# Attention in steps of two: maxima subtracted by four 32-row matmuls, and score banks shared in turn

## The chip, the cores and the metric

The kernel runs on one core of a Trainium2 chip. A core has five engines that run side by side, each with its own queue executed in program order: TensorE (PE) multiplies matrices, VectorE (DVE) and ScalarE (ACT) do arithmetic and read TensorE's results, GpSimd (POOL) does arithmetic on SBUF, SyncE (SP) starts DMAs. Results of TensorE land in PSUM, which has eight banks of 128 partitions x 512 float32 numbers. The metric is the device time of one launch in microseconds (us), median of several runs.

## The reference

The reference has two layers on an input of shape (4, 128, 64, 64), float32. Layer 0 is attention over the 4096 positions of each image, with 4 heads of width 32, followed by a residual and a layer norm over the channels. Layer 1 sums a 3x3 convolution, a spectral 1x1 convolution (through a 2-D Fourier transform) and a selective scan ("Mamba": 256 inner channels, 16 states).

```
Q, K, V = split_heads(x_flat @ W + b)
attn = softmax(einsum("bhnd,bhmd->bhnm", Q, K) * head_dim ** -0.5)
y = layernorm((attn @ V merged) @ Wo + bo + x_flat)
out = conv3x3(y) + spectral(y) + mamba(y)
```

The change is in how the softmax's scores are formed: the row maximum has to be known before the exponential is taken, so the kernel forms all scores twice, once to find the maxima and once, with the maximum subtracted, for the exponential.

## The kernel before

**Tiles.** The positions of an image are cut into 8 chunks of 512 queries. A "half" H is one chunk of queries with one pair of heads, so there are 64 halves. Within a half there are 32 steps, one for each block of 128 keys. That makes 2048 steps in all, and time in the kernel's program is counted in these steps (`t`).

**One step** issues, in this order:

- `scores_for_exp`(H, m), line 486: scores of 128 keys x 512 queries for both heads of the pair, into a tile of two PSUM banks (tag `s2`, one buffer). Each head has its own bank and its own 64 rows of TensorE's array, so the two heads' matmuls stand side by side. Three such pairs of matmuls are summed: queries in a low and a high part (K times Q), then the negated maximum, added by a matmul of `sel` (ones in two rows of each head's 64) with `MX`, which holds the negated maxima in a high and a low part in those two rows. ScalarE takes the exponential of the two banks at once (line 502).
- `scores_for_max`(H + 1, s), line 442: scores of 128 queries x 512 keys for the next half, two pairs of matmuls into two banks (tag `s1`, one buffer), reduced to a maximum per query by VectorE (line 461). It runs `LEAD` = 7 steps ahead of the next half's first exponential.
- `times_values`(H, m - 1), line 505: the exponentials of the step before times V, for the two heads in two column halves of the array, summed in one bank (tag `o`). These are plain float32 and each takes two instructions.

After the last step of a half, ScalarE and VectorE each copy one head's sums out of the bank (`oz`, lines 524 and 525). `maxima` (line 463) takes the last maximum over the parts, splits it, writes it to `wide` and has TensorE transpose it into `MX`.

**Side work.** Projections, the layer norm, the convolution, the spectral part and the scan of earlier chunks run in the gaps. `Plan` (line 102) holds them as jobs that give way at each need: P for a place on TensorE, D on VectorE, A on ScalarE, B for one of two shared PSUM banks (`m0`, `m1`). `plan.step` is called once per step with the number of places; before the change a step with an odd number gives two places of each kind and an even one gives one to ScalarE only. The scan is issued outside the planner: in every second step one state is scanned by VectorE (`scan_state`, line 834), with its decay from ScalarE (`scan_decay`, line 821, into a bank of its own) and its products on GpSimd (lines 832, 854, 873). When the attention is over, a remainder of the scan runs alone.

PSUM is full: two banks for `s1`, two for `s2`, and one each for `o`, `dA`, `m0`, `m1`. A tile with one buffer can be written again only when its reader is done.

The loop that sets the order is the last of the function, from line 1062:

```
if 0 <= H < HALVES:
    scores_for_exp(H, m)
h1, s1 = divmod(t + LEAD, NT)
if 0 <= h1 + 1 < HALVES:
    scores_for_max(h1 + 1, s1)
...
plan.step(t, {"D": 2, "P": 2, "A": 2})
...
if not last and 0 <= H < HALVES:
    times_values(H, m)
```

Of the kernel before, what the change touches and what calls it, by code (L numbers as in the profile page):

```python
# [9 lines left out]
F32 = mybir.dt.float32  # L10
F32R = mybir.dt.float32r
AF = mybir.ActivationFunctionType
ALU = mybir.AluOpType
# [4 lines left out]
P = 128  # L18
W = 64
HEADS = 4  # L20
HD = P // HEADS
PAIRS = HEADS // 2
HS = P // 2
L = 512
RPC = L // W
TPC = L // P
# [25 lines left out]
def _constants():  # L52

    w = np.arange(W)
    k = np.arange(1, W // 2)
    sin = np.sin(2 * np.pi * np.outer(w, k) / W).sum(1) * 2 / W
    hil = sin[(w[:, None] - w[None, :]) % W]
    c = np.zeros((P, NCONST), np.float64)
    c[:, K_ID : K_ID + P] = np.eye(P)  # L70
    for r in range(2):
        s = slice(r * W, (r + 1) * W)
        c[s, K_HIL + r * W : K_HIL + (r + 1) * W] = hil.T
    c[:, K_G : K_G + W] = -sin
    for j in range(2):
        c[j * HS, K_SEL : K_SEL + P] = 1.0
        c[j * HS + HD, K_SEL : K_SEL + P] = 1.0
    c[2 * DTR : 4 * DTR, K_LO] = -1.0
    for j in range(2):
        c[(2 * j + 1) * DTR : (2 * j + 2) * DTR, K_LO + 1] = -1.0  # L80
    return c.astype(np.float32)
# [80 lines left out]
def attention_then_conv_mamba(  # L162
# [153 lines left out]
    ]  # L316
    VA = [const.tile([P, TPC, HEADS, HD + 1], F32, name=f"V_{i}") for i in range(NCH)]

    wide = const.tile([P, TPC, 2, HS], F32, name="wide")
    nc.gpsimd.memset(wide, 0.0)  # L320
    state = const.tile([P, NH * NS], F32, name="state")
    carry = const.tile([P, NH, TAPS - 1], F32, name="carry")
# [119 lines left out]
    def scores_for_max(H, s):  # L442

        k = H % PAIRS
        m, t = divmod(s, TPC)
        assert have["K", k, m] == H // PAIRS // NCH
        if s == 0:
            part[H] = att.tile([P, TPC, 2, NCH], F32, tag="part", name=f"part_{H}")

        tag = "s2" if H == 0 and s % 2 else "s1"  # L450
        sc = psum.tile([P, 2, L], F32, tag=tag, name=f"s1_{H}_{s}")
        for n in range(2):
            for j in range(2):
                nc.tensor.matmul(  # L454
                    sc[:, j, :],
                    QT[H][rows[j], n, t * P : (t + 1) * P],
                    KK[k][m][rows[j], :],
                    start=n == 0,
                    stop=n == 1,
                )  # L460
        nc.vector.tensor_reduce(part[H][:, t, :, m], sc, AX.X, ALU.max)  # L461

    def maxima(H):

        yield "D"
        mx = att.tile([P, TPC, 2], F32, tag="mx", name=f"mx_{H}")
        nc.vector.tensor_reduce(mx, part.pop(H), AX.X, ALU.max)
        hi = att.tile([P, TPC, 2], F32R, tag="mhi", name=f"mhi_{H}")
        nc.vector.tensor_scalar(hi, mx, -1.0, None, ALU.mult)
        nc.vector.tensor_copy(wide[:, :, :, 0], hi)  # L470
        nc.vector.scalar_tensor_tensor(wide[:, :, :, HD], mx, -1.0, hi, ALU.mult, ALU.subtract)
        yield ""
        bank = yield "PB"
        pm = bank_tile(bank, [P, L], f"pm_{H}")
        for t in range(TPC):
            nc.tensor.transpose(
                pm[:, t * P : (t + 1) * P], wide[:, t].rearrange("p j d -> p (j d)"), ident
            )
        yield "A"
        plan.release(bank)  # L480
        MX[H] = att.tile([P, L], F32R, tag="MX", name=f"MX_{H}")
        nc.scalar.activation(MX[H], pm, AF.Copy)
# [2 lines left out]

    def scores_for_exp(H, m):

        k = H % PAIRS
        i, t = divmod(m, TPC)
        assert have["K", k, i] == H // PAIRS // NCH  # L490
        s = psum.tile([P, 2, L], F32, tag="s2", name=f"s2_{H}_{m}")
        for n, mov in enumerate((QT[H][:, 0, :], QT[H][:, 1, :], MX[H])):
            for j in range(2):
                nc.tensor.matmul(  # L494
                    s[:, j, :],
                    sel[rows[j], :] if n == 2 else KK[k][i][rows[j], t * P : (t + 1) * P],
                    mov[rows[j], :],
                    start=n == 0,
                    stop=n == 2,
                )  # L500
        e = att.tile([P, 2, L], F32, tag="e", name=f"e_{H}_{m}", bufs=3)
        nc.scalar.activation(e, s, AF.Exp)  # L502
        es[H, m] = e

    def times_values(H, m):

# [314 lines left out]
    def scan_decay(c, v):  # L821
        n, hf = divmod(v, NH)
        k = hf * NS + n

        tag = "o" if plan.t >= HALVES * NT + 2 and v % 2 else "dA"
        dA[c, v] = psum.tile([P, L], F32, tag=tag, name=f"dA_{c}_{k}")
        nc.scalar.activation(dA[c, v], dts[c][hf], AF.Exp, scale=negA[:, k : k + 1])  # L827

    def scan_input_term(c, v, engine):
        n, hf = divmod(v, NH)  # L830
        db[c, v] = loc.tile([P, L], F32, tag="db", name=f"db_{c}_{hf * NS + n}")
        engine.tensor_tensor(db[c, v], us[c][hf], bcs[c, n][0], ALU.mult)  # L832

    def scan_state(c, v):

        n, hf = divmod(v, NH)
        k = hf * NS + n
        assert (c, hf) in scaled
        late = plan.t > HALVES * NT + 1
        if late:  # L840
            hs = flat(VA[v % 4])
        else:
            hs = loc.tile([P, L], F32, tag="hs", name=f"hs_{c}_{k}")
        nc.vector.tensor_tensor_scan(  # L844
            hs,
            dA.pop((c, v)),
            db.pop((c, v)),
            state[:, k : k + 1] if c % NCH else zero,
            ALU.mult,
            ALU.add,  # L850
        )
        if c % NCH < NCH - 1:
            nc.gpsimd.tensor_copy(state[:, k : k + 1], hs[:, L - 1 :])  # L853
        nc.gpsimd.tensor_tensor(hs, hs, bcs[c, n][1], ALU.mult)  # L854
        if hf == NH - 1 and (c, n) in taken:
            spare.append((plan.t + 6, taken.pop((c, n))))
        elif hf == NH - 1:
            ring[0] += 1
        if late:

            if c not in sums_late:
                sums_late[c] = psum.tile(
                    [P, NH, L], F32, tag=f"s{1 + c % 2}", name=f"acc_{c}"
                )
            terms = [hs] if n else [xss[c][hf], hs]
            for x in terms:
                waiting.append((plan.t + 4, c, hf, x, n == NS - 1 and x is hs))
        elif n == 0:
            acc = loc.tile([P, L], F32, tag=f"acc{hf}", name=f"acc_{c}_{hf}")
            accs[c, hf] = acc  # L870
            nc.gpsimd.tensor_tensor(acc, xss[c][hf], hs, ALU.add)
        else:
            nc.gpsimd.tensor_tensor(accs[c, hf], accs[c, hf], hs, ALU.add)  # L873
# [149 lines left out]

    LEAD = 7
    SLOT = PAIRS * NT
    LAG = 2 * SLOT + 16
    STATES = NH * NS
# [26 lines left out]
        for i in range(NCH // 2):  # L1056
            plan.at((b + 1) * NCH * SLOT + 44 + 10 * i, 4, flips(b * NCH + NCH // 2 - 1 - i))

    t = 6 - SLOT
    loaded = 0  # L1060
    end = (CHUNKS + 3) * SLOT
    while t < end or not plan.idle():
        H, m = divmod(t, NT)
        if 0 <= H < HALVES:
            scores_for_exp(H, m)
        h1, s1 = divmod(t + LEAD, NT)
        if 0 <= h1 + 1 < HALVES:
            scores_for_max(h1 + 1, s1)
        H, m = divmod(t - 1, NT)
        last = m == NT - 1  # L1070
        if last and 0 <= H < HALVES:
            times_values(H, m)
        c, s = divmod(t - LAG, SLOT)
        odd = s % 2 == 1
        if -1 <= c < CHUNKS:
            v = c * STATES + s // 2
            if not odd:
                if v >= 0:
                    scan_state(*divmod(v, STATES))
            else:  # L1080
                if 0 <= v + 1 < CHUNKS * STATES:
                    scan_decay(*divmod(v + 1, STATES))
                if 0 <= v + 2 < CHUNKS * STATES:
                    late = t > HALVES * NT
                    scan_input_term(
                        *divmod(v + 2, STATES), nc.vector if late else nc.gpsimd
                    )

                if loaded < CHUNKS * NS and loaded // NS in bcds:
                    if ring[0] or spare and spare[0][0] <= t:  # L1090
                        scan_load(*divmod(loaded, NS))
                        loaded += 1
        plan.late = t > HALVES * NT
        if plan.late:
            add_states()
            if odd:
                plan.step(t, {"D": 4, "P": 4, "A": 6})
            plan.t = t
        elif t < -LEAD:
            plan.step(t, {"D": 4, "P": 4, "A": 4})  # L1100
        elif odd:
            plan.step(t, {"D": 2, "P": 2, "A": 2})
        else:
            plan.step(t, {"D": 0, "P": 0, "A": 1})
        if not last and 0 <= H < HALVES:
            times_values(H, m)
        t += 1


# [74 lines left out]
```

## Time and profile before

| | us |
|---|---|
| median of 3 runs | 6039.58 (6039.44 to 6041.75) |
| the profiled execution | 6038.33 |
| its span | 6036.5 |
| TensorE busy | 5847.1 (97%) |
| VectorE busy | 4360.0 (72%) |
| ScalarE busy | 3586.6 (59%) |
| GpSimd busy | 4482.6 (74%) |
| attention: first to last matmul of L494 and L514 | 128.5 to 5817 |

A group in the profile is all instructions of one line, engine and tile; "idle before" is the time the engine stood still just before them. A wait line reads "engine line <- engine line waited for: us in total, times, longest". A timeline row has start, length, engine, line, operation, out<-in and how many instructions it merges. A matmul's recorded length overlaps that of the next, so intervals between starts tell more than lengths. The granted clock of TensorE is full (1.00) from 300 to 5700 us.

### The profile page before, as it was taken

The numbers are of one execution on the slowest core, as the hardware profiler recorded it, in microseconds if no ns is written. First come the engines' busy times: TensorE is split into PE (matmuls) and PEld (weight loads), VectorE is DVE, ScalarE is ACT, GpSimd is POOL, SyncE is SP. The second block draws the span as 40 slices with busy tenths as digits, with TensorE's granted clock in tenths as the row PEclk, the third lists the DMA queues.
The fourth block names the chain that finished last, engine by engine and source line by source line (L and its number), as shares of the span: only waits on it lengthen the run. The fifth ranks groups of instructions, "written<-read, shape, count | busy, mean of one in ns | idle before, by whom it ended". The sixth has DMA issues, their size and how long they took to land. (4 is left out here: it accounts for less than half of the span.)

```text
span 6036.5 us, 82731 instructions
## 1 busy us (share of the span) xinstructions
PE 5847.1 (97%) x31382; PEld 2443.1 (40%) x31382; DVE 4360.0 (72%) x4569; ACT 3586.6 (59%) x4826; POOL 4482.6 (74%) x4522
## 2 busy tenths in 40 slices
PE   5999999999999999999999999999999999999976
PEld 2444444444444444444444444444444444444422
DVE  4557777777777777777777777777777777777657
ACT  1455666666666666666666666666666666666653
POOL 0006888778887778888788888777888887888877
PEclk7999999999999999999999999999999999999988
DMA  4012222224333223223432222322433222222233
GB/s 125 25 36 58 65 71 75 71 70 110 82 89 73 73 72 74 72 64 89 104 84 82 74 68 71 75 68 73 108 75 92 67 67 63 66 71 63 62 98 89
DMA packets 266641, 455.28 MB, mean 75 GB/s; under 512 B 46688, under 2 KB 48256, under 8 KB 266240
## 3 DMA queue, kind: packets, MB, share of 16 engines
q1 hardware_dynamic: 261584, 448.11, 28.1%
q8 instruction: 246, 4.03, 0.3%
q10 hardware_dynamic: 4656, 1.87, 0.1%
q14 instruction: 155, 1.27, 0.1%
HBM read 375.68 MB, written 65.80 MB: 73 GB/s over the span
## 5 line engine op out<-in xcount | busy, mean ns | idle before, releaser
L461 DVE TENSOR_REDUCE part<-s 128x2 f32<-128x1024 f32 x2048 | 2498.1, 1221 | 1411.4 <-PE s L454 1407.6
L502 ACT ACTIVATE e<-s 128x1024 f32<-128x1024 f32 x2048 | 2095.5, 1023 | 2121.6 <-PE s L494 2117.0
L514 PE MATMUL po<-e,V 128*33 128x512 f32 x8192 | 2180.9, 605 | 2.4 <-DVE oz L525 0.3
L494 PE MATMUL s<-Q,K 64*128 64x512 f32 x8192 | 1501.0, 444 | 13.5 <-ACT e L502 10.2
L454 PE MATMUL s<-K,Q 64*128 64x512 f32 x8192 | 1308.9, 397 | 41.4 <-DVE part L461 32.3
L854 POOL TENSOR_TENSOR hs<-hs,bc 128x512 f32<-128x512 f32 x948 | 1211.0, 1277 | 170.3 <-DVE hs L844 101.3
L494 PEld LDWEIGHTS s<-Q,K 64*128 64x128 f32 x8192 | 610.2, 185 | 1736.3 <-ACT e L502 1237.0
L832 POOL TENSOR_TENSOR db<-u,bc 128x512 f32<-128x512 f32 x948 | 1215.6, 1282 | 0.0
L873 POOL TENSOR_TENSOR acc<-acc,hs 128x512 f32<-128x512 f32 x894 | 1145.4, 1281 | 70.1
L844 DVE TENSOR_TENSOR_SCAN hs<-dA,state,db 128x512 f32<-128x512 f32 x826 | 1052.8, 1275 | 41.9 <-ACT dA L827 40.1
L454 PEld LDWEIGHTS s<-K,Q 64*128 64x128 f32 x8192 | 750.1, 185 | 294.9 <-DVE part L461 129.4
L494 PE MATMUL s<-MX,sel 64*128 64x512 f32 x4096 | 808.0, 391 | 0.0
L827 ACT ACTIVATE dA<-dt,negA 128x512 f32<-128x512 f32 x1024 | 703.2, 687 | 115.7 <-DVE V L844 69.5
L853 POOL COPY state<-hs 128x1 f32<-128x1 f32 x858 | 157.9, 184 | 789.8 <-DVE hs L844 786.0
L514 PEld LDWEIGHTS po<-e,V 128*33 128x33 f32 x8192 | 305.4, 109 | 886.5 <-issue 840.8
L494 PEld LDWEIGHTS s<-MX,sel 64*128 64x128 f32 x4096 | 383.9, 185 | 90.7
L928 PE MATMUL pf<-xp,cw 128*128 128x512 f32 x576 | 288.2, 618 | 0.0
L558 POOL TENSOR_TENSOR op<-op,rz 128x512 f32<-128x512 f32 x32 | 41.4, 1294 | 178.6 <-DMA rz<-rd 175.8
L844 DVE TENSOR_TENSOR_SCAN hs<-dA,zero,db 128x512 f32<-128x512 f32 x128 | 163.2, 1275 | 0.9 <-POOL db L832 0.7
L880 PE MATMUL acc<-V,cst 128*128 128x512 f32 x140 | 95.0, 783 | 63.6 <-POOL V L854 63.5
L928 PEld LDWEIGHTS pf<-xp,cw 128*128 128x128 f32 x576 | 96.8, 189 | 119.6 <-issue 117.9
L712 POOL TENSOR_TENSOR xs<-xs,sg_x 128x512 f32<-128x512 f32 x64 | 81.8, 1279 | 79.3 <-ACT sg_x L636 79.3
(147 smaller groups left out, 3571.2 us busy)
## 6 DMA issues: line engine op xcount, KB each, us to landing
bc<-bcd SPq DMA_DIRECT2D x487, 512.0 KB
Q<-qd SPq DMA_DIRECT2D x256, 128.0 KB
K<-kd SPq DMA_DIRECT2D x64, 256.0 KB
K<-bcd SPq DMA_DIRECT2D x42, 256.0 KB
vd<-vst SPq DMA_DIRECT2D x32, 264.0 KB
V<-vd SPq DMA_DIRECT2D x32, 264.0 KB
xq<-in_x SPq DMA_DIRECT2D x32, 256.0 KB
xk<-in_x SPq DMA_DIRECT2D x32, 256.0 KB
```

The lines of the kernel that those rows point to most:

```text
L454: nc.tensor.matmul(sc[:, j, :], QT[H][rows[j], n, t * P : (t + 1) * P], KK[k][m][rows[j], :], start=n == 0, stop=n == 1,)
L461: nc.vector.tensor_reduce(part[H][:, t, :, m], sc, AX.X, ALU.max)
L494: nc.tensor.matmul(s[:, j, :], sel[rows[j], :] if n == 2 else KK[k][i][rows[j], t * P : (t + 1) * P], mov[rows[j], :], start=n == 0, stop= ...
L502: nc.scalar.activation(e, s, AF.Exp)
L514: nc.tensor.matmul(po[H][used[j], :], VA[i][:, t, 2 * k + j, :], e[:, j, :], start=m == 0, stop=m == NT - 1,)
L827: nc.scalar.activation(dA[c, v], dts[c][hf], AF.Exp, scale=negA[:, k : k + 1])
L832: engine.tensor_tensor(db[c, v], us[c][hf], bcs[c, n][0], ALU.mult)
L844: nc.vector.tensor_tensor_scan(hs, dA.pop((c, v)), db.pop((c, v)), state[:, k : k + 1] if c % NCH else zero, ALU.mult, ALU.add,)
L853: nc.gpsimd.tensor_copy(state[:, k : k + 1], hs[:, L - 1 :])
L854: nc.gpsimd.tensor_tensor(hs, hs, bcs[c, n][1], ALU.mult)
L873: nc.gpsimd.tensor_tensor(accs[c, hf], accs[c, hf], hs, ALU.add)
L928: nc.tensor.matmul(pf, cw[:, k, :], xps[c][:, dy : dy + RPC, dx : dx + W], start=k == 0, stop=False)
```

## The change

Two steps are issued together. `scores_for_exp` fills two tiles: the scores of the first step, then four matmuls of 32 rows each that add the negated maxima (`sel` now has ones in the first two rows of each 32; `wide` and so `MX` hold the high and low part in each quarter), then the scores of the second step. Quarter q = 0 of each head goes to the first tile and closes its sum, q = 1 goes to the second tile and opens its sum. The tags `s1` and `s2` become `s0` and `s1`, and maxima scores and exponential scores of even steps share `s0`, those of odd steps `s1`. The loop is written anew for pairs of steps: both exponentials, the values of the step before, the maxima scores of the even step, side work with places for TensorE, the maxima scores of the odd step, the values, side work with places for VectorE, then the scan. `LEAD` is 8.

```diff
-    for j in range(2):
-        c[j * HS, K_SEL : K_SEL + P] = 1.0
-        c[j * HS + HD, K_SEL : K_SEL + P] = 1.0
+    for r in range(P // HD):
+        c[r * HD : r * HD + 2, K_SEL : K_SEL + P] = 1.0
...
-    wide = const.tile([P, TPC, 2, HS], F32, name="wide")
+    wide = const.tile([P, TPC, 2, 2, HD], F32, name="wide")
...
-        tag = "s2" if H == 0 and s % 2 else "s1"
-        sc = psum.tile([P, 2, L], F32, tag=tag, name=f"s1_{H}_{s}")
+        sc = psum.tile([P, 2, L], F32, tag=f"s{s % 2}", name=f"s1_{H}_{s}")
...
-        nc.vector.tensor_copy(wide[:, :, :, 0], hi)
-        nc.vector.scalar_tensor_tensor(wide[:, :, :, HD], mx, -1.0, hi, ALU.mult, ALU.subtract)
+        high, low = (wide[:, :, :, :, k] for k in range(2))
+        mx2, hi2 = (v.unsqueeze(3).to_broadcast([P, TPC, 2, 2]) for v in (mx, hi))
+        nc.vector.tensor_copy(high, hi2)
+        nc.vector.scalar_tensor_tensor(low, mx2, -1.0, hi2, ALU.mult, ALU.subtract)
...
+        both = [
+            psum.tile([P, 2, L], F32, tag=f"s{r}", name=f"s2_{H}_{m + r}") for r in range(2)
+        ]
+        for r in range(2):
+            i, t = divmod(m + r, TPC)
+            for n in range(2):
+                for j in range(2):
+                    nc.tensor.matmul(
+                        both[r][:, j, :],
+                        KK[k][i][rows[j], t * P : (t + 1) * P],
+                        QT[H][rows[j], n, :],
+                        start=n == 0 and r == 0,
+                        stop=n == 1 and r == 1,
+                    )
+            if r == 0:
+                for j in range(2):
+                    for q in range(2):
+                        quarter = slice(j * HS + q * HD, j * HS + (q + 1) * HD)
+                        nc.tensor.matmul(
+                            both[q][:, j, :],
+                            sel[quarter, :],
+                            MX[H][quarter, :],
+                            start=q == 1,
+                            stop=q == 0,
+                        )
+            e = att.tile([P, 2, L], F32, tag="e", name=f"e_{H}_{m + r}", bufs=3)
+            nc.scalar.activation(e, both[r], AF.Exp)
+            es[H, m + r] = e
...
-    LEAD = 7
+    LEAD = 8
...
+    for t in range(6 - SLOT, ATTENTION + 2, 2):
+        plan.t = t
+        if 0 <= t < ATTENTION:
+            scores_for_exp(*divmod(t, NT))
+        values(t - 1)
+        max_scores(t)
+        decay(t)
+        early = t < -LEAD
+        plan.step(t, {"D": 4, "P": 4, "A": 4} if early else {"D": 0, "P": 2, "A": 1})
+        max_scores(t + 1)
+        values(t)
+        plan.step(t + 1, {"D": 4, "P": 4, "A": 4} if early else {"D": 2, "P": 0, "A": 2})
+        scan(t)
+        prepare(t + 1, nc.gpsimd)
...
+    while not plan.idle() or t < (CHUNKS + 3) * SLOT:
+        plan.t = t
+        decay(t)
+        scan(t)
+        add_states()
+        decay(t + 2)
+        prepare(t + 1, nc.vector)
+        add_states()
+        plan.step(t + 1, {"D": 4, "P": 4, "A": 6})
+        t += 2
```

More of the change, by code (lines that the diff above doesn't have):

```diff
@@ L476, in maxima @@
             nc.tensor.transpose(
-                pm[:, t * P : (t + 1) * P], wide[:, t].rearrange("p j d -> p (j d)"), ident
+                pm[:, t * P : (t + 1) * P], wide[:, t].rearrange("p j r d -> p (j r d)"), ident
             )
@@ L488, in scores_for_exp @@
         k = H % PAIRS
[L489 to L503, printed above, removed]
+        both = [
[3 more added lines that the diff above has]
+            i, t = divmod(m + r, TPC)
+            assert have["K", k, i] == H // PAIRS // NCH
+            for n in range(2):
[21 more added lines that the diff above has]
+            es[H, m + r] = e
     def times_values(H, m):
@@ L862, in scan_state @@
                 sums_late[c] = psum.tile(
-                    [P, NH, L], F32, tag=f"s{1 + c % 2}", name=f"acc_{c}"
+                    [P, NH, L], F32, tag=f"s{c % 2}", name=f"acc_{c}"
                 )
@@ L1057, in attention_then_conv_mamba, with decay, scan, prepare @@
             plan.at((b + 1) * NCH * SLOT + 44 + 10 * i, 4, flips(b * NCH + NCH // 2 - 1 - i))
-    t = 6 - SLOT
     loaded = 0
[L1061 to L1065, printed above, removed]
+    decayed = -1
+    def decay(t):
+        nonlocal decayed
+        v = (t - LAG) // 2
+        if 0 <= v < CHUNKS * STATES and v > decayed:
+            scan_decay(*divmod(v, STATES))
+            decayed = v
+    def scan(t):
+        v = (t - LAG) // 2
+        if 0 <= v < CHUNKS * STATES:
+            scan_state(*divmod(v, STATES))
+    def prepare(t, engine):
+        nonlocal loaded
+        v = (t - LAG) // 2 + 2
+        if 0 <= v < CHUNKS * STATES:
+            scan_input_term(*divmod(v, STATES), engine)
+        if loaded < CHUNKS * NS and loaded // NS in bcds:
+            if ring[0] or spare and spare[0][0] <= t:
+                scan_load(*divmod(loaded, NS))
+                loaded += 1
+    def max_scores(t):
         h1, s1 = divmod(t + LEAD, NT)
@@ L1068, in attention_then_conv_mamba, with values @@
             scores_for_max(h1 + 1, s1)
-        H, m = divmod(t - 1, NT)
-        last = m == NT - 1
-        if last and 0 <= H < HALVES:
+    def values(t):
+        H, m = divmod(t, NT)
+        if 0 <= H < HALVES:
             times_values(H, m)
[L1073 to L1107, printed above, removed]
+    ATTENTION = HALVES * NT
@@ L1111 @@
+    plan.late = True
+    t = ATTENTION + 2
+    while not plan.idle() or t < (CHUNKS + 3) * SLOT:
[8 more added lines that the diff above has]
+        t += 2
 def kernel(**inputs):
```

## The prediction, made before the changed kernel ran

> **What bounds the kernel now.** I read the busy table first, then the groups and the waits, then the timeline of one step. TensorE is 97% busy, but a matmul's ends are modelled, so I ask who waits for whom.
>
> ```profile
> PE 5847.1 (97%) x31382; PEld 2443.1 (40%) x31382; DVE 4360.0 (72%) x4569; ACT 3586.6 (59%) x4826; POOL 4482.6 (74%) x4522
> ...
> ACT e L502 <- PE s L494: 2117.0, 1860, 9.7
> DVE part L461 <- PE s L454: 1407.6, 860, 11.3
> ...
> PE s L454 <- DVE part L461: 32.3, 62, 1.5
> ```
>
> ScalarE and VectorE wait thousands of microseconds for TensorE's scores. TensorE waits 32 us in all for VectorE. So TensorE's own queue sets the pace of the attention, and I price that queue matmul by matmul. The timeline (start, length, engine, line) shows one step without side work, then one with a matmul of 32 rows:
>
> ```profile
> 3007.25 0.73 PE L494 MATMUL s<-Q,K 64*128 64x512 f32 x4
> 3007.82 0.39 PE L494 MATMUL s<-MX,sel 64*128 64x512 f32 x2
> 3008.05 0.62 PE L454 MATMUL s<-K,Q 64*128 64x512 f32 x4
> 3008.61 1.05 PE L514 MATMUL po<-e,V 128*33 128x512 f32 x4
> 3009.59 0.50 PE L494 MATMUL s<-Q,K 64*128 64x512 f32 x2
> ...
> 3663.46 0.63 PE L454 MATMUL s<-K,Q 64*128 64x512 f32 x4
> 3664.02 0.72 PE L742 MATMUL pdt<-dtr,dtw 32*128 32x512 f32 x2
> 3664.67 1.05 PE L514 MATMUL po<-e,V 128*33 128x512 f32 x4
> ```
>
> Starts, not lengths, are what counts. A pair of 64-row matmuls side by side ("a pass") takes 0.23 (3007.82 to 3008.05). Two passes before a change of shape take 0.56 (3008.05 to 3008.61), so 0.10 is lost at the change. Two passes just after a change take 0.57: 0.11 is a weight load that could not go ahead. The values take 0.98. A clean step is 2.34. L742 is the key row: two matmuls on 32 rows, following 64-row ones. The change to it costs the usual 0.10 (3663.46 to 3664.02 is 0.56), and its own two matmuls take 0.65 = 2 x 0.23 + 0.10 for the load + 0.10 for the next change. So going from 64 to 32 rows is a full change of shape, worth about 0.20.
>
> VectorE matters too. These are its reductions at the start, where nothing but they and the maxima's matmuls run, and one clean step:
>
> ```profile
> 85.69 0.73 PE L454 MATMUL s<-K,Q 64*128 64x512 f32 x4 [0.27 <-DVE part L461]
> 86.82 0.73 PE L454 MATMUL s<-K,Q 64*128 64x512 f32 x4 [0.40 <-DVE part L461]
> ...
> 3008.32 1.02 ACT L502 ACTIVATE e<-s 128x1024 f32<-128x1024 f32 x1 [1.32 <-PE s L494]
> 3008.72 1.23 DVE L461 TENSOR_REDUCE part<-s 128x2 f32<-128x1024 f32 x1
> ```
>
> Back-to-back reductions follow each other at 1.13 to 1.14; one lasts 1.23; the matmuls into its bank start 0.05 after its end. The reduction begins 0.44 after its last pass starts (3008.28 to 3008.72), an exponential 0.50 after (3007.82 to 3008.32).
>
> **What the Trainium skill says.** "TensorEngine Tiling (Array Packing)", Key Properties: "Changing tiling mode (not just tile) drains the TensorE". The trace agrees, 0.10 at each change. "TensorE: Matmul & The Clock Gate", Part 3: four 32-row matmuls on different row groups run together, 3.07 times as fast as one after the other; here only pairs are seen (starts 0.003 apart), so four are taken as one pass. The same part says that a weight load overlaps a running matmul only where its row group differs; in this trace loads on the same rows are hidden (0.23 a pass), except after a change, and I follow the trace. "PSUM — Partial Sum Buffer", bank collisions: two engines may not be in one bank at once, so a bank pair passes from matmul to reader and back by waits. The trace has such waits (L454 on L461).
>
> **The change, part by part.** In program order TensorE now runs, for two steps: scores A (two passes, 64 rows), four 32-row maxima, scores B, values, maxima scores 0, side work, maxima scores 1, values. Of 1024 pairs of steps 586 have side work, 438 have none (counted in the new program order; before, 598 single steps had it).
>
> 1. *Maxima.* Two passes become one: -0.23 a pair. Two changes of shape come in (64 to 32, 32 to 64): 2 x 0.20 = +0.40. A clean pair goes from 4.68 to 4.85, x 1024: +174 us.
> 2. *Side work moved* from between 64-row scores and values (a change stood there anyway) to between two 64-row groups: one more change, 0.20 x 586 = +117 us.
> 3. *Banks in turn: a new wait.* The second quarter matmul is the first into bank pair 1, so it waits for the reduction of maxima scores 1; behind it in TensorE's strict order stand the rest of the quarters, both exponentials' scores and the values. Take that start as 0. Maxima 0.11+0.23+0.10, B 0.57+0.10, values 0.98, first pass of maxima scores 0 with its load 0.34: the second pass starts at 2.42. Reduction 0 starts at 2.86 (+0.44), reduction 1 at 4.00 (+1.14), ends at 5.23, and the next quarter starts at 5.27. TensorE alone needs 4.85. With side work maxima 1 come later, but TensorE then needs 4.85 plus at least 0.8 (four transposes: 0.32+0.16+0.22+0.20 less 0.23, plus the load 0.11), so there TensorE and not the reduction ends last: only the 438 clean pairs wait, 5.27 - 4.85 = 0.41 each: +180 us. Other buffers are in time: pair 0 is free of its exponential at 1.63 and wanted at 2.08, pair 1 at 2.6 and wanted at 2.65.
> 4. *VectorE before reduction 0* has 2.86 less the scan (1.19) and up to two side jobs of 0.68: enough. It is not where a half ends: ScalarE's copy of `oz` (0.59) is now behind both exponentials and VectorE's (0.70) behind it, so reduction 0 starts about 0.85 late, 63 times; and not at long jobs (maxima 0.21+0.34+0.31+1.04 = 1.9; statistics 2.4). Where such a pair is clean it loses 0.7 to 0.9; I take 45 us, ends 0 and 110.
> 5. *Doubled `wide`, LEAD 8, start and end.* Copies of 8 elements become 16: nothing (VectorE row 0.31). One more reduction ahead (+1.1), but the seven maxima steps before the first exponential now alternate banks (2.3 to 1.1 a step): -5 us. The end loop issues the scan, the decay and the products in the same order as before: 0. The planner's places per pair are as before (2 for VectorE, 2 for TensorE, 3 for ScalarE), so side work neither gathers nor thins; SP and POOL issue the same work and the same DMAs, and POOL, about 80% busy, gets more time per pair. Were that cover gone, POOL's three products of 1.28 a pair would show only below 4.4.
>
> Sum: 174 + 117 + 180 + 45 - 5 = +511. The profiled execution took 6038.3 (span 6036.5), the median is 6039.6; on the median that gives 6550 us.
>
> **Rivals.** *Row change free* (for: the four array strips are separate; against: L742). Pair 4.45, but the chain of point 3 is still 4.96: 438 x 0.28 + 586 x (-0.03) + 40 = +145: 6185. *Quarters one after the other in two pairs* (against: the skill's 3.07; for: no run here has four): +0.23 x 1024 more, 6785. *The reductions' wait hidden* (if the second pair's reading ends early enough): without points 3 and 4, 6325. *Faster: the quarters slip in beside their neighbours.* If different row groups need no drain and the quarters overlap the 64-row passes, the whole maxima step costs q near 0 instead of 0.63. Then a side-work pair is 4.68 - 0.46 + q + 0.20, and a clean one, held by the chain, 4.73 + q. Over all: 586 x (q - 0.26) + 438 x (q + 0.05) + 40 = 1024 q - 90: faster below q = 0.09, and 5950 at q = 0. Against it: 0.10 lost at all 64-to-32 changes seen.
>
> **How the numbers follow.** Forecast 0.76; row change free 0.08; quarters serial 0.07; wait hidden 0.05; faster 0.04. The forecast's own range is 6450 to 6640 (a change of shape worth 0.16 to 0.24 moves it by some 80; point 4 by 50 to 65). Both neighbours at 6325 and part of the dear ones make it 6320 to 6670. Of the chances, faster by over 0.2% (about what a measurement of this kernel can tell) gets 0.04, the same 0.02 (q near 0.09), slower 0.94.
>
> **What would show it.** In the timeline after: scores A, quarters and B start 0.67, then 0.43 apart where nobody waits; four quarter matmuls start within 0.02 in job pairs, while in clean pairs the first goes alone and the others 0.05 after a reduction's end. A clean pair is near 5.26, a new wait of TensorE on the reduction stands at about 180 us with loads included, and VectorE's wait for L454's successor shrinks. Quarters followed by B after 0.23 would refute the row change's price; a clean pair of 4.85 the wait; two quarters 0.23 behind the other two the concurrency. Any slowdown of VectorE or ScalarE rows themselves would be none of these.

## The result and the profile after

The changed kernel takes 6478.75 us (6478.03 to 6479.31), the kernel before 6039.51 in the runs beside it: a ratio of 1.0727 (95% interval 1.0708 to 1.0745), 439 us slower. The forecast was 6550, in a range of 6320 to 6670.

The busy table and the waits of the changed kernel (its L451, L497, L508, L516, L528 are the maxima scores, the exponentials' scores, the quarters, the exponential and the values):

```profile
PE 6283.8 (97%) x31384; PEld 2195.6 (34%) x31384; DVE 4315.7 (67%) x4568; ACT 3518.9 (54%) x4826; POOL 4472.9 (69%) x4522
...
ACT e L516 <- PE s L508: 2488.3, 1021, 5.9
DVE part L458 <- PE s L451: 1911.6, 1392, 10.8
...
PEld s L508 <- DVE part L458: 97.8, 430, 0.8
...
PEld po L528 <- DVE oz L539: 57.0, 62, 2.5
...
PE po L528 <- DVE oz L539: 29.7, 62, 1.6
```

TensorE's share is 97% as before; a busy share can't show the loss, because waits and changes of shape are covered by modelled matmul lengths. ScalarE and VectorE wait longer for TensorE than they did (2488 against 2117 us and 1912 against 1408). New is that the quarters wait for a reduction, 430 times, which is nearly the count of clean pairs, those without side work (438). The reduction is that of the pair before, so the wait falls into the pair that follows a clean one. A wait's total counts only the time in which the weight loader stood idle just before, so intervals between starts measure it better. The timeline after: a pair whose quarters wait, with the loads of these quarters, and a later pair whose quarters don't.

```profile
3008.76 0.73 PE L497 MATMUL s<-Q,K 64*128 64x512 f32 x4
3009.43 0.92 PE L508 MATMUL s<-MX,sel 32*128 32x512 f32 x4
3010.27 0.73 PE L497 MATMUL s<-Q,K 64*128 64x512 f32 x4
3010.94 1.05 PE L528 MATMUL po<-e,V 128*33 128x512 f32 x4
...
3009.43 0.18 PEld L508 LDWEIGHTS s<-MX,sel 32*128 32x128 f32 x1 [0.37 <-issue]
3009.84 0.19 PEld L508 LDWEIGHTS s<-MX,sel 32*128 32x128 f32 x3 [0.23 <-DVE part L458]
...
3016.15 0.73 PE L497 MATMUL s<-Q,K 64*128 64x512 f32 x4
3016.81 0.50 PE L508 MATMUL s<-MX,sel 32*128 32x512 f32 x4
3017.24 0.73 PE L497 MATMUL s<-Q,K 64*128 64x512 f32 x4
```

In the later pair the scores of the first step (A), the quarters and the scores of the second step (B) start 0.66 and 0.43 apart: the four quarters are one pass (their starts are 0.003 apart), but they need 0.43 where a 64-row pass took 0.23. In the first pair one quarter goes at 3009.43 and the other three at 3009.84, after the reduction of the second maxima group. VectorE has two reductions in a row there:

```profile
3007.43 2.36 DVE L458 TENSOR_REDUCE part<-s 128x2 f32<-128x1024 f32 x2 [1.11 <-PE s L451]
3009.70 1.28 DVE L858 TENSOR_TENSOR_SCAN hs<-dA,state,db 128x512 f32<-128x512 f32 x1
```

They end at 3009.79; the quarters' loads restart 0.05 later. All of the loss lies in the attention: from the first matmul that adds the negated maxima to the last values it went from 5687 us (129.3 to 5816.7) to 6127 us (124.4 to 6251.7), +440, with -5 before it and +5 after it.

### The profile page after: what moved, and what is told of

It is laid out like the page before. It is cut to its first block, busy times and chain, and to the rows that moved or that the text cites. A ratio compares the mean times of both kernels' runs of the same rounds, so it can differ in the third digit from the quotient of the medians.

```text
span 6476.2 us, 82757 instructions
## 1 busy us (share of the span) xinstructions
PE 6283.8 (97%) x31384; PEld 2195.6 (34%) x31384; DVE 4315.7 (67%) x4568; ACT 3518.9 (54%) x4826; POOL 4472.9 (69%) x4522
## 5 line engine op out<-in xcount | busy, mean ns | idle before, releaser
L458 DVE TENSOR_REDUCE part<-s 128x2 f32<-128x1024 f32 x2048 | 2469.4, 1224 | 1918.4 <-PE s L451 1911.6
L516 ACT ACTIVATE e<-s 128x1024 f32<-128x1024 f32 x2048 | 1986.8, 1022 | 2488.6 <-PE s L508 2488.3
L528 PE MATMUL po<-e,V 128*33 128x512 f32 x8192 | 2157.1, 605 | 29.8 <-DVE oz L539 29.7
L497 PE MATMUL s<-Q,K 64*128 64x512 f32 x8192 | 1502.0, 444 | 12.5 <-DVE part L458 12.5
L451 PE MATMUL s<-K,Q 64*128 64x512 f32 x8192 | 1399.6, 436 | 13.4 <-DVE part L458 12.6
L451 PEld LDWEIGHTS s<-K,Q 64*128 64x128 f32 x8192 | 615.2, 185 | 1285.1 <-ACT e L516 917.7
L497 PEld LDWEIGHTS s<-Q,K 64*128 64x128 f32 x8192 | 610.9, 185 | 1126.0 <-issue 660.6
L508 PE MATMUL s<-MX,sel 32*128 32x512 f32 x4096 | 693.1, 495 | 0.3 <-DVE part L458 0.3
L528 PEld LDWEIGHTS po<-e,V 128*33 128x33 f32 x8192 | 299.3, 109 | 787.5 <-issue 719.3
L508 PEld LDWEIGHTS s<-MX,sel 32*128 32x128 f32 x4096 | 272.6, 181 | 473.0 <-issue 375.1
```

Of the source, the lines that this page charges most:

```text
L451: nc.tensor.matmul(sc[:, j, :], QT[H][rows[j], n, t * P : (t + 1) * P], KK[k][m][rows[j], :], start=n == 0, stop=n == 1,)
L497: nc.tensor.matmul(both[r][:, j, :], KK[k][i][rows[j], t * P : (t + 1) * P], QT[H][rows[j], n, :], start=n == 0 and r == 0, stop=n == 1 an ...
L508: nc.tensor.matmul(both[q][:, j, :], sel[quarter, :], MX[H][quarter, :], start=q == 1, stop=q == 0,)
L516: nc.scalar.activation(e, both[r], AF.Exp)
L528: nc.tensor.matmul(po[H][used[j], :], VA[i][:, t, 2 * k + j, :], e[:, j, :], start=m == 0, stop=m == NT - 1,)
```

## The experiments

**A change of rows alone, in the kernel before.**

```diff
+    top = [slice(j * HS, j * HS + HD) for j in range(2)]
...
-                    sel[rows[j], :] if n == 2 else KK[k][i][rows[j], t * P : (t + 1) * P],
-                    mov[rows[j], :],
+                    sel[top[j], :] if n == 2 else KK[k][i][rows[j], t * P : (t + 1) * P],
+                    mov[top[j] if n == 2 else rows[j], :],
```

The ones of `sel` now stand in the first two rows of each head's 64, and the low part of the maxima in the second of them, so that all of it lies in the 32 rows used.

> The kernel before with one thing done: in every step the negated maxima are added by two matmuls of 32 rows (rows 0-31 and 64-95) in place of two of 64 rows; same number of passes, same order, same banks. Theory (a change between 64 and 32 rows costs as much as any change of shape, 0.10 for the drain and 0.10 for the weight load): two changes more in each of 2048 steps, +0.40 each, +820 us less some 60 us of stalls that the longer step swallows: 6780 to 6860. Rival 'the row change is free': 6040. Rival 'only the drain is paid': +0.20 a step, about 6430.

Measured 6764.02 us, ratio 1.1198 (1.1181 to 1.1214), +724. Its timeline of one step:

```profile
3004.04 0.73 PE L494 MATMUL s<-Q,K 64*128 64x512 f32 x4
3004.70 0.49 PE L494 MATMUL s<-MX,sel 32*128 32x512 f32 x2
3005.12 0.73 PE L454 MATMUL s<-K,Q 64*128 64x512 f32 x4
3005.78 0.62 PE L514 MATMUL po<-e,V 128*33 128x512 f32 x2
```

The starts are 0.66, 0.42 and 0.66 apart where they were 0.57, 0.23 and 0.56 before. With 0.98 for the values that is 2.73 a step (the median of the steps without side work) against 2.34: two changes cost 0.39, 0.19 to 0.20 each, nearly all of the price taken from L742. Over 2048 steps that would be 790 (the last 39 steps have no maxima scores and pay about half). I expected some 60 back from stalls. A stall is counted here as the time by which an interval between two starts exceeds the usual interval between matmuls of these two kinds; summed, the stalls of TensorE's queue go down from 92 to 24 us, and 790 - 68 = 722. Both rivals (free, or the drain alone) are refuted.

**64-row maxima in the changed kernel.**

```diff
-                for j in range(2):
-                    for q in range(2):
-                        quarter = slice(j * HS + q * HD, j * HS + (q + 1) * HD)
+                for q in range(2):
+                    for j in range(2):
...
-                            sel[quarter, :],
-                            MX[H][quarter, :],
+                            sel[rows[j], :],
+                            MX[H][rows[j], :],
```

The ones of `sel` stand only in the first two rows of each head's 64. Both heads' matmuls for the first tile now come first, so one whole pass goes ahead of the wait.

> The changed kernel with the four 32-row maxima matmuls replaced by two pairs of 64 rows (one pass more, no change of shape); order, banks and waits as in the changed kernel. Theory (the row changes cost more than the saved pass gives, both in the queue and in the chain over the reductions): the pairs of steps with side work 0.17 shorter, 586 x 0.17 = 100; the clean pairs' chain 5.27 becomes 4.96, 438 x 0.31 = 136; 6479 - 236 = 6243. Rival 'the reductions' wait is what costs, and it hides the row changes': only the pairs with side work gain, 6380. Rival 'row changes are free': one pass more, 6479 + 135 = 6614.

Measured 6292.85, ratio 1.0417 (1.0400 to 1.0434): 186 less than the changed kernel, between the theory's 236 and the rival's 99. The weight loader of a waiting pair shows why:

```profile
3010.70 0.19 PEld L507 LDWEIGHTS s<-MX,sel 64*128 64x128 f32 x2
3011.44 0.19 PEld L507 LDWEIGHTS s<-MX,sel 64*128 64x128 f32 x2 [0.55 <-DVE part L458]
3011.55 0.43 PEld L497 LDWEIGHTS s<-Q,K 64*128 64x128 f32 x4
```

The load of the waiting matmul waits too (3011.44, just after the reduction), so its 0.11 is exposed after the wait, here without a change of rows. My 4.96 for the chain had left it out. With it the chain is 5.07, and 5.071 is the median of the clean pairs; 438 x 0.20 + 586 x 0.17 = 187 against 186 measured. So the theory holds with that size put right, and the rival that the wait hides the row changes is 87 us short.

**Side work after both maxima groups.**

```diff
-        plan.step(t, {"D": 4, "P": 4, "A": 4} if early else {"D": 0, "P": 2, "A": 1})
         max_scores(t + 1)
+        plan.step(t, {"D": 4, "P": 4, "A": 4} if early else {"D": 0, "P": 2, "A": 1})
         values(t)
```

> The changed kernel with the side work's place moved from between the two maxima groups to between the second maxima group and the values, where a change of shape stands anyway. Theory: 586 pairs lose one change of 0.20, -117: 6362. The reductions come no later, since the pairs with side work are longer than the 5.27 of the chain anyway. Rival 'the place of the side work costs nothing': 6479. Rival 'side work between the maxima was hiding part of the wait for bank pair 1': slower than 6479.

Measured 6370.94, ratio 1.0549 (1.0534 to 1.0565): 108 less, for 117 expected. A pair with side work in the changed kernel, then one in this run:

```profile
3011.92 0.74 PE L451 MATMUL s<-K,Q 64*128 64x512 f32 x4
3012.59 1.13 PE L411 MATMUL pq<-xq,wq_t 128*128 128x512 f32 x2
3013.55 1.02 PE L797 MATMUL pz<-xp,inw 128*128 128x512 f32 x2
3014.50 0.73 PE L451 MATMUL s<-K,Q 64*128 64x512 f32 x4
3015.16 1.05 PE L528 MATMUL po<-e,V 128*33 128x512 f32 x4
...
3009.12 1.24 PE L451 MATMUL s<-K,Q 64*128 64x512 f32 x8
3010.29 1.98 PE L1003 MATMUL py<-acc,outw 128*128 128x512 f32 x4
3012.21 1.05 PE L528 MATMUL po<-e,V 128*33 128x512 f32 x4
```

Apart, the two maxima groups take 0.67 and 0.66 to the next start; together they take 1.17. The pairs with side work are 0.18 shorter on average (6.53 to 6.35), the clean ones unchanged (5.27 and 5.26). The place of the side work alone cost a quarter of the slowdown.

**Half of the reductions' work left out**, in the changed kernel and, as a control, in the kernel before.

```diff
-        nc.vector.tensor_reduce(part[H][:, t, :, m], sc, AX.X, ALU.max)
+        nc.vector.tensor_reduce(part[H][:, t, :, m], sc[:, :, : L // 2], AX.X, ALU.max)
```

> The changed kernel with VectorE's maxima taken over half of the keys only (256 of 512 columns), which leaves half of that work out and makes each reduction about 0.5 us shorter; TensorE's queue is the same. Theory (432 pairs wait 0.41 for the second reduction): the waits before the second quarter matmul vanish, -176, and some 15 to 25 us at the ends of halves: about 6285. A clean pair becomes 4.85. Rival 'the clean pairs are held by ScalarE's exponentials or by TensorE': less than 50 us gained.

> The kernel before with VectorE's maxima over half of the keys only (half of that work left out), as a control. Theory (TensorE sets the pace, 92 us of its queue are stalls, some 65 of them before the maxima scores that wait for a late reduction): 5965 to 5995. Rival 'TensorE never waits for VectorE before the change': 6040 within 5.

Changed kernel: 6276.89, ratio 1.0393 (1.0377 to 1.0408), 202 less. Kernel before: 5987.13, 0.9913 (0.9898 to 0.9928), 52 less. The groups and the timeline of the changed kernel with half of that work left out:

```profile
L458 DVE TENSOR_REDUCE part<-s 128x2 f32<-128x512 f32 x2048 | 1379.1, 690 | 2763.5 <-PE s L451 2760.9
...
3002.47 0.73 PE L497 MATMUL s<-Q,K 64*128 64x512 f32 x4
3003.12 0.50 PE L508 MATMUL s<-MX,sel 32*128 32x512 f32 x4
3003.55 0.73 PE L497 MATMUL s<-Q,K 64*128 64x512 f32 x4
3004.22 1.05 PE L528 MATMUL po<-e,V 128*33 128x512 f32 x4
3005.20 0.73 PE L451 MATMUL s<-K,Q 64*128 64x512 f32 x4
```

A reduction is now 0.69 long, and the quarters go together right after a clean pair as well (0.43 to the next scores); no wait of theirs for a reduction is left in the list of waits. The median clean pair is 4.90, against the 4.85 that TensorE's queue alone was worked out to need. The cost of that queue itself, row changes and moved side work, remains: 6277 against 5987 of the control, 290 us, where 174 + 117 = 291 had been worked out.

**Two and three things undone.** First the 64-row maxima and the moved side work together, then also half of the reductions left out.

> The changed kernel with two things undone: 64-row maxima, and the side work after the second maxima group. What remains is the order in pairs and the banks shared in turn. Theory (costs add up): 6243 - 117 = 6126, 6120 to 6165; still slower than before by the reductions' wait in the clean pairs (438 x 0.28 = 123) and by the ends of halves. Rival 'the pair order costs nothing by itself': 6040.

> As the run with 64-row maxima and the side work moved, and with the maxima over half of the keys (half of that work left out), so that no wait for a reduction is left. Theory: about 5990, within 20 us of the kernel before with the same half left out: nothing of the slowdown remains that the three causes don't explain. Rival 'a further cost of the pair order': over 6020.

Measured 6172.88, ratio 1.0220 (1.0205 to 1.0235), and 5997.23, ratio 0.9929 (0.9914 to 0.9944). The first is 8 us above the range named; with the chain at 5.07 instead of 4.96, 48 us more would have been expected than the 6126 named. It shows that the order in pairs with shared banks, without the quarters, loses 133 us, the waits at the ends of halves among them. The second is 10 us above the kernel before with the same half left out, where 20 were allowed. Of its own stalls 31 us stand at the ends of halves. So the three causes account for all but some 10 us, and `LEAD`, the wider `wide` and the new loop, which are all still in this kernel, cost no more than that.

**Quarters last.** One change of shape less.

```diff
...
+        for j in range(2):
+            for q in range(2):
+                quarter = slice(j * HS + q * HD, j * HS + (q + 1) * HD)
+                nc.tensor.matmul(
+                    both[q][:, j, :], sel[quarter, :], MX[H][quarter, :], start=False, stop=True
+                )
+        for r in range(2):
             e = att.tile([P, 2, L], F32, tag="e", name=f"e_{H}_{m + r}", bufs=3)
```

The scores now open the sums of both tiles, and the quarters close them.

> The changed kernel with the four 32-row matmuls put after the scores of both steps, in front of the values: one change of shape less a pair (64 to 32 to values, in place of 64 to 32 to 64 to values). Both exponentials can now start only after them. Theory (the chain over banks decides in the clean pairs): the first exponential ends 1.68 after the quarters start, the values end 1.41 after, so the first maxima group waits 0.27; the clean pairs' chain is 5.55, the pairs with side work are 4.92 plus theirs in place of 4.85: 438 x 0.28 + 586 x 0.07 = +164, 6640. Rival 'the number of changes decides': 586 x -0.20 = -117, 6362 or less.

Measured 6628.82, ratio 1.0974 (1.0956 to 1.0992): 150 slower than the changed kernel, for 161 expected, and not 117 faster. The timeline:

```profile
3024.38 0.51 PE L507 MATMUL s<-MX,sel 32*128 32x512 f32 x4
3024.82 1.05 PE L524 MATMUL po<-e,V 128*33 128x512 f32 x4
3024.99 1.94 ACT L512 ACTIVATE e<-s 128x1024 f32<-128x1024 f32 x2 [2.68 <-PE s L507]
3026.07 0.73 PE L451 MATMUL s<-K,Q 64*128 64x512 f32 x4 [0.19 <-ACT e L512]
```

The values take 0.98, so the maxima scores could go at 3025.80; they go at 3026.07, when the first exponential has left the bank pair: 0.27, as worked out (in nearly all pairs this wait is 0.20 or 0.27). In the clean pairs that follow a clean one the second maxima group then waits a further 0.35 for the second exponential. Fewer changes don't help where both exponentials start late and hand their banks over late. The median of all clean pairs is 5.48, of those that follow a clean one 5.53, for the 5.55 named.

**The ends of halves.**

```diff
+        if t % NT == 0:
+            values(t - 1)
         if 0 <= t < ATTENTION:
             scores_for_exp(*divmod(t, NT))
-        values(t - 1)
+        if t % NT:
+            values(t - 1)
```

> The changed kernel with the last values of each half (64 of 2048 steps) issued before the next half's first pair of scores, so that the two copies of the sums come ahead of the exponentials on ScalarE; all else the same. Theory (the copies behind both exponentials hold VectorE's reduction and the next values up, 50 us of TensorE's stalls at 62 ends of halves): those stalls go, -50; two changes of shape less at each end, -0.4, but the first maxima group then follows scores B and waits some 0.7 for the first exponential, +18 in all: 6430 to 6450. Rival 'the ends of halves cost nothing beyond the chain': 6479 or slower.

Measured 6446.93, ratio 1.0673 (1.0655 to 1.0691): 32 less, inside the range named. The 50 us of stalls after `oz` (33 before the values, 17 before scores A) are gone from the intervals.

## Why the prediction was right, and where it was off

**What sets the pace** (TensorE's queue, priced by starts): right. Leaving out half of the reductions' work gives the kernel before 52 us and no more.

**Step 1, the maxima**, +174: right in its rule, that the pass saved (0.23) is less than two row changes. The price 0.20 read from L742 measured 0.19 to 0.20 in a run of its own. That four quarters share one pass, which the trace of before could not show, holds: 0.43 with load and drain, as was summed. The pair without waits needs 4.86 by its usual intervals, for 4.85 worked out.

**Step 2, the moved side work**, +117: measured 108.

**Step 3, the new wait**, +180: right in its place, count and size. The clean pair was worked out as 5.27 and has a median of 5.267; 432 waits of about 0.41 sum to some 176. That the wait falls away behind a pair with side work was right too: the 301 clean pairs that follow a clean one have a median of 5.275, the 130 that follow a pair with side work 4.907. The other waits are in pairs with side work that follow a clean one.

**Step 4, ends of halves and long side jobs**, +45: the ends measured 50 of stalls, and undoing them brought 32 net of the waits that this makes itself; the long side jobs can hardly be seen. The cause, copies of `oz` behind both exponentials, was right, and so was the loss of about 0.8 an end. The place was only half right: the late reduction 0 costs 0.27 before the next scores A, while the larger part, 0.53, stands before the second values, which wait for VectorE's copy to leave the bank `o` (62 waits for L539 in the list). The prediction did not name that wait, so that its total came near is partly luck.

**Step 5**: -5 at the start was measured (the first matmul that adds the negated maxima starts at 124.4 in place of 129.3); the end is 5 longer, for 0.

**The size that was off** is the sum: it was put on top of the measured time of before as if all of that kernel's stalls stayed. By the intervals between starts TensorE's queue had 92 us of stalls before: 47 and 18 at the maxima scores, which waited for a late reduction, 22 before the exponentials' scores, 4 elsewhere. In the longer pair these are swallowed: what is left after is 176 before the quarters, 50 at the ends, 10 before the second maxima group. So the stalls' own balance is 236 - 92 = 144 and not 180 + 45 = 225. With it, 174 + 117 + 144 = 435, against 440 measured in the attention. The prediction had read the 32 us by which matmuls waited for VectorE in the list of waits and left them alone; it should have priced them, together with the weight loader's part (129 us in the same list, not all of it on the path), as a thing that the change removes.

**The rivals.** A free row change and a change that costs only its drain are refuted by the row change alone (the first one's chain of 4.96 also left out the 0.11 for the load after a wait, as the run with 64-row maxima showed); serial quarters by the 0.43; the hidden wait by the 202 us less the control's 52. The mechanism of the faster case (q near 0) is refuted by the same 0.43: q is 0.63 with the drain before and the exposed load after.

## What to carry to other kernels

Price TensorE's queue by the starts of its matmuls, with a fixed charge for each change of shape (here about 0.2 us for 64 to 32 rows or back), and count the changes in program order: a packed pass pays only if it saves more than the changes it brings (here 0.23 against 0.39). Two tiles in turn over four banks look like double buffering, but when two users share them in turn, a chain goes round once per pair (here quarters, scores B, values, first maxima scores, two reductions, and the next quarters), and it has to be shorter than the queue. When a step grows, add up also the stalls of the old schedule that it will swallow.

## What the runs showed of the hardware

A waiting matmul's weight load waits with it: in the run with 64-row maxima, the pass that waited for a reduction (433 times) was followed by the next after 0.34, where 0.23 is usual, so each of these waits exposed 0.11 more. I had put this in for the 32-row matmuls and forgotten it for 64-row ones that follow others of the same shape. Row changes cost the same whether two or four 32-row matmuls follow (0.42 and 0.43 to the next group).
